# One pipeline over both images in layer 1, with the norms and copies moved into running work

## The chip, the cores and the metric

The kernel runs on one core of a Trainium2 chip, as one program. The time is the device time of one execution in microseconds (us). The core has a matrix engine (TensorE, PE in the profile; PEld is its loading of weights), a vector engine (VectorE, DVE), an engine for functions of one operand (ScalarE, ACT), a general engine (GpSimd, POOL) and an engine that here only issues transfers (SyncE, SP). Each engine works through its own queue in order. ScalarE can issue transfers too; such an issue stands in its queue between its other instructions.

## The reference

Two layers, each with a residual, on an input of 2 images of 64 x 64 places with 256 channels, all in float32:

```
x = x + L0(gn(x))        # gn: normalise over groups of 8 channels and all places of an image
x = x + L1(gn(x))

L0: mamba scans of rows (mh) and of columns (mv), each forward and backward:
    xz = x @ in_w.T;  xi, z = split(xz)
    xi = silu(conv4(xi)); dt, B, C = split(xi @ x_w.T); dt = softplus(dt @ dt_w.T + b)
    h_t = exp(dt*A) * h_{t-1} + dt*xi*B ;  y_t = sum_n h_t*C    # 16 states, 512 channels
    out = ((y + xi*D) * silu(z)) @ out_w.T ; the four results are joined by fc_w

L1: for i in 0, 1:
        x = x + mamba2(rmsnorm(x))   over columns ("t" weights of layer i)
        x = x + mamba2(rmsnorm(x))   over rows    ("b" weights of layer i)
    mamba2: one product with Win, conv4 and silu, decays exp(cumsum) as 64 x 64 matrices
            for 8 heads, both directions, gate, rmsnorm, product with Wout
```

L1 is four calls of mamba2 in a row; each needs the whole image of the call before, since columns and rows take turns. The two images never meet.

## The kernel before

Channels lie on the 128 partitions, in two groups (`KT`); an image is a tile of 128 x 2 x 4096. Two such tiles are held: `XU` (the layer's input, and in layer 1 the running `U`) and `Y` (layer 0's result).

A block is four rows or columns of 64 places (`TB` = 256 places); an image has 16 (`NBLK`). All work is cut into steps of a block. Lists such as `STEPS0` (layer 0) and `STEPS` (layer 1) give each step a due time within a block; `plan` adds block number times period, and `issue` sorts all steps by due time and emits them. So the order on every engine is written out by these numbers, and `pin` (keep in program order) fixes it. One block has a period of 3200 units in layer 0 (a step of the scan each 100) and of 100 in layer 1. Instructions that are not pinned may be moved by the framework that places the waits: the transfers of layer 1, and `group_norm` with what surrounds the calls there.

**Layer 0** (`layer0`) is one pipeline of 64 blocks: image 0 rows, image 0 columns, image 1 rows, image 1 columns. Per block and state, ScalarE makes the decay (L391), GpSimd the inflow (L741) or the product with C (L771), VectorE the scan (L760) or the product (L774), TensorE the sum over states (L398). The rows of B and C come from DRAM (`b_row`, `c_row`, issued by SyncE). Image 1's tile takes the place of image 0's as soon as the last `norm_x` (L570) of image 0 has read it: eight transfers (L418), issued one after the other on ScalarE's queue, then 16 `bn_stats` (L426) on VectorE and a chain of small operations to the factors `gscale` and `gshift`. Image 0's result is written to DRAM (`y_kept`, L471), likewise eight transfers one after the other on ScalarE's queue. `residual` (L854, L864) ends a block.

**Layer 1** (`layer1`) is called twice, image 1 in `Y` first, then image 0. It begins with `group_norm` (L336 to L355) and writes the normalised `Y` into `U` (L936, 16 instructions). Then come four calls, each with its own loading and scaling of weights (L950 to L991, the pool has two buffers of each), and its own `issue` of 16 blocks. In a block: `norm_squares` (ScalarE), `norm_total` (GpSimd, L1045), `norm_mean` (TensorE), `norm_factor`, `norm_scale` (VectorE, L1057, writes `xn`), projections (TensorE, L930), convolution (ScalarE L927, VectorE L1018), decays (GpSimd L1162, TensorE, ScalarE), `outputs` (TensorE), `gated` (VectorE L1269), the second norm and projection, `residual` (GpSimd L1314). In the fourth call `residual` also adds `U` to `Y` (L1317), writes the output from `Y`, and for the first of the two images loads the other's `Y` back from `y_kept` (L1320) into the same place.

Of the kernel before, what the change touches and what calls it, by code (L numbers as in the profile page):

```python
# [134 lines left out]
    (-8799, "load"),  # L135
    (-7899, "stats", 0),
    (-7824, "stats", 1),
    (-7749, "stats", 2),
    (-7674, "stats", 3),
    (-7599, "stats", 4),  # L140
    (-7524, "stats", 5),
    (-7449, "stats", 6),
    (-7374, "stats", 7),
    (-7299, "stats", 8),
    (-7224, "stats", 9),
    (-7149, "stats", 10),
    (-7074, "stats", 11),
    (-6999, "stats", 12),
    (-6924, "stats", 13),
    (-6849, "stats", 14),  # L150
    (-6774, "stats", 15),
    (-6629, "moments"),
    (-6554, "mean_sum"),
    (-6479, "mean_dev"),
    (-6404, "var_sum"),
    (-6329, "factor"),
    (-6254, "offset"),
)
SPILL = 899
# [58 lines left out]
    (460, "out_scale"),  # L218
    (559, "residual"),
)  # L220

# [7 lines left out]
def seqs(ap):  # L229

    return ap.rearrange("p (s l) -> p s l", l=L)
# [97 lines left out]
def group_norm(nc, k, pool, psum, src):  # L329

    n = NTOK // 512
    stats = pool.tile([P, KT, n, 6], F32, name="gn_stats")
    moments = pool.tile([P, KT, 2], F32, name="gn_moments")
    for kt in range(KT):
        for j in range(n):
            nc.vector.bn_stats(stats[:, kt, j, :], src[:, kt, j * 512 : (j + 1) * 512])  # L336
        nc.vector.bn_aggr(moments[:, kt, :], stats[:, kt, :, :].rearrange("p n s -> p (n s)"))
    mean = pool.tile([P, KT], F32, name="gn_mean")
    nc.vector.tensor_copy(mean, moments[:, :, 0])
    pm = psum.tile([P, 512], F32, name="ps_mm")  # L340
    nc.tensor.matmul(pm[:, 0:KT], lhsT=k.gavg, rhs=mean, start=True, stop=True)
    gmean = pool.tile([P, KT], F32, name="gn_gmean")
    nc.vector.tensor_copy(gmean, pm[:, 0:KT])
    spread = pool.tile([P, KT], F32, name="gn_spread")
    nc.vector.tensor_sub(spread, mean, gmean)
    nc.vector.tensor_mul(spread, spread, spread)
    nc.vector.tensor_add(spread, spread, moments[:, :, 1])
    pv = psum.tile([P, 512], F32, name="ps_mm")
    nc.tensor.matmul(pv[:, 0:KT], lhsT=k.gavg, rhs=spread, start=True, stop=True)
    std = pool.tile([P, KT], F32, name="gn_std")  # L350
    nc.scalar.activation(std, pv[:, 0:KT], AF.Sqrt, bias=k.eps_gn)
    scale = pool.tile([P, KT], F32, name="gn_scale")
    nc.vector.reciprocal(scale, std)
    shift = pool.tile([P, KT], F32, name="gn_shift")
    nc.vector.scalar_tensor_tensor(shift, gmean, -1.0, scale, ALU.mult, ALU.mult)  # L355
    return scale, shift


def layer0(tc, k, d, big, x, kept_ctx):
# [11 lines left out]
    with ExitStack() as ctx:  # L371
# [35 lines left out]
        class Image:  # L407


            def __init__(self, b):  # L410
                self.b, self.Y = b, None

            def load(self):
                self.X = big.tile([P, KT, NTOK], F32, name="XU")
                for j in range(NTOK // 512):
                    t = slice(j * 512, (j + 1) * 512)
                    queue = nc.scalar if self.b else nc.sync
                    pin(queue.dma_start(out=self.X[:, :, t], in_=x[self.b][:, :, t]))  # L418

            def stats(self, i):  # L420
                n = NTOK // 512
                if i == 0:
                    self.st = small.tile([P, KT, n, 6], F32, name="gn_stats")
                kt, j = i % KT, i // KT
                t = slice(j * 512, (j + 1) * 512)
                pin(nc.vector.bn_stats(self.st[:, kt, j, :], self.X[:, kt, t]))  # L426

            def moments(self):
                self.mom = small.tile([P, KT, 2], F32, name="gn_moments")
                for kt in range(KT):  # L430
                    st = self.st[:, kt, :, :].rearrange("p n s -> p (n s)")
                    pin(nc.vector.bn_aggr(self.mom[:, kt, :], st))
                self.mean = small.tile([P, KT], F32, name="gn_mean")
                pin(nc.vector.tensor_copy(self.mean, self.mom[:, :, 0]))

            def mean_sum(self):
                self.pm = ps_mm.tile([P, 512], F32, name="ps_mm")
                matmul(self.pm[:, 0:KT], k.gavg, self.mean, True, True)

            def mean_dev(self):  # L440
                self.gmean = small.tile([P, KT], F32, name="gn_gmean")
                pin(nc.vector.tensor_copy(self.gmean, self.pm[:, 0:KT]))
                self.spread = small.tile([P, KT], F32, name="gn_spread")
                pin(nc.vector.tensor_sub(self.spread, self.mean, self.gmean))
                pin(nc.vector.tensor_mul(self.spread, self.spread, self.spread))
                pin(nc.vector.tensor_add(self.spread, self.spread, self.mom[:, :, 1]))

            def var_sum(self):
                self.pv = ps_mm.tile([P, 512], F32, name="ps_mm")
                matmul(self.pv[:, 0:KT], k.gavg, self.spread, True, True)  # L450

            def factor(self):

                log = small.tile([P, KT], F32, name="gn_log")
                act(log, self.pv[:, 0:KT], AF.Ln, bias=k.eps_gn)
                self.gscale = small.tile([P, KT], F32, name="gn_scale")
                act(self.gscale, log, AF.Exp, scale=-0.5)

            def offset(self):
                self.gshift = small.tile([P, KT], F32, name="gn_shift")  # L460
                pin(
                    nc.vector.scalar_tensor_tensor(
                        self.gshift, self.gmean, -1.0, self.gscale, ALU.mult, ALU.mult
                    )
                )

            def spill(self):
                self.kept = big_dram(tc, kept_ctx, [P, KT, NTOK], f"y_kept{self.b}")
                for j in range(NTOK // 512):
                    t = slice(j * 512, (j + 1) * 512)  # L470
                    pin(nc.scalar.dma_start(out=self.kept[:, :, t], in_=self.Y[:, :, t]))  # L471
# [394 lines left out]
        images = [Image(b) for b in range(n_img)]  # L866
# [18 lines left out]
        todo += plan(images[1:], 2 * period * NBLK, shifted(IMAGE0, 2 * period * NBLK), -4)  # L885
        spill = [(2 * period * NBLK + SPILL, "spill")]
        todo += plan(images[:-1], 2 * period * NBLK, spill, -4)

        images[0].load()
# [6 lines left out]
        for _, name, *args in IMAGE0[1:]:  # L896
            getattr(images[0], name)(*args)
# [9 lines left out]
        return images[-1].Y, [image.kept for image in images[:-1]]  # L907


def layer1(tc, k, d, U, Y, out, after):  # L910
# [6 lines left out]
    with ExitStack() as ctx:  # L917
# [14 lines left out]
        gscale, gshift = group_norm(nc, k, small, ps, Y)  # L932
        for j in range(NTOK // 512):
            for kt in range(KT):
                t = slice(j * 512, (j + 1) * 512)
                nc.vector.tensor_scalar(  # L936
                    U[:, kt, t],
                    Y[:, kt, t],
                    gscale[:, kt : kt + 1],
                    gshift[:, kt : kt + 1],  # L940
                    ALU.mult,
                    ALU.add,
                )

        for call in range(4):
            ax, li = "tb"[call % 2], call // 2
            axis = "vh"[call % 2]

            w_in = wp.tile([P, KT, PROJ], F32, name="w_in")
            nc.sync.dma_start(out=w_in, in_=d[ax + "_Win"][li])  # L950
            w_out = wp.tile([P, CT, C], F32, name="w_out")
            nc.sync.dma_start(out=w_out, in_=d[ax + "_Wout"][li])
            norm_w = wp.tile([P, KT], F32, name="norm_w")
            nc.sync.dma_start(out=norm_w, in_=d[ax + "_norm_w"][li])

            cols = wp.tile([P, CT, TAPS + 3], F32, name="cols")
            nc.sync.dma_start(out=cols, in_=d[ax + "_cols"][li])
            bc_cols = wp.tile([P, TAPS + 1], F32, name="bc_cols")
            for j in range(2):
                nc.sync.dma_start(  # L960
                    out=bc_cols[j * NS1 : (j + 1) * NS1, :], in_=d[ax + "_bc_cols"][li][:, j, :]
                )
# [40 lines left out]
            def bank():  # L1003
                return ps.tile([P, 512], F32, name="ps_mm")
# [394 lines left out]
```

## Time and profile before

Three runs took 8777.42, 8782.16 and 8782.59 us; the median is 8782.16. The profiled execution has a span of 8783.1 us.

| | whole span | 5000 to 5100 us (layer 0) | 6450 to 6500 us (layer 1) |
|---|---|---|---|
| TensorE busy | 91% | 89.0% | 100% |
| its weight loads | 75% | 76.1% | 79.0% |
| VectorE | 87% | 97.7% | 75.1% |
| ScalarE | 80% | 84.7% | 80.3% |
| GpSimd | 89% | 99.9% | 77.7% |
| granted TensorE clock | 0.956 | 0.98 | 1.00 |
| moved by DMA | 109 GB/s | 149 GB/s | 1 GB/s |

How it is read: the shares of the whole span mix two stages with different limits, so each stage has to be read by itself. A busy TensorE is not TensorE at its peak, for matmuls overlap and their ends are modelled. Where one engine's instruction repeats once a block, its starts give the time of a block. "idle <- X" behind an instruction names what ended the wait of its engine.

Layer 0 lasts until its last `residual` starts at 6263.2 us; the rest is layer 1.

### The profile page before, as it was taken

How to read it: one execution, taken by the hardware profiler on the slowest of the kernel's cores; microseconds unless marked ns; L12 is line 12 of the kernel's file. 1: busy time of each engine (PE TensorE's matmuls, PEld its weight loads, DVE VectorE, ACT ScalarE, POOL GpSimd, SP SyncE). 2: the span in 40 equal slices, each digit the busy share in tenths (PEclk: the TensorE clock that was granted, in tenths of full speed). 3: DMA queues.
4: the chain of work that ended last, by engine and by line, in shares of the span. 5: the costliest groups of instructions: out<-in, count | busy, mean ns of one | idle time of the engine just before them, and what ended most of it. 6: DMA issues, size and time to landing. Idle time of an engine off the chain costs nothing. (4 is left out here: it accounts for less than half of the span.)

```text
span 8783.1 us, 150445 instructions
## 1 busy us (share of the span) xinstructions
PE 7950.0 (91%) x55632; PEld 6598.0 (75%) x55632; DVE 7651.9 (87%) x7433; ACT 7016.0 (80%) x12062; POOL 7787.5 (89%) x4494
## 2 busy tenths in 40 slices
PE   8989989898998889989988998998799999899999
PEld 6777777777777777777777777777677777677777
DVE  7999999999999989999999999999876666667666
ACT  6888888888888778888888888888577776677777
POOL 7999999999999899999999999999676666667667
PEclk9999999999999999999999999999899999999999
DMA  5444554544545554444554445555200000100000
GB/s 154 149 146 146 148 150 146 151 148 147 146 148 147 151 160 148 146 149 148 148 150 147 146 149 148 145 148 148 75 7 4 9 1 25 31 9 1 9 4 18
DMA packets 531631, 955.65 MB, mean 109 GB/s; under 512 B 71056, under 2 KB 83856, under 8 KB 528848
## 3 DMA queue, kind: packets, MB, share of 16 engines
q1 hardware_dynamic: 523568, 928.71, 36.0%
q10 hardware_dynamic: 7328, 17.31, 0.5%
q8 instruction: 440, 7.21, 0.3%
q14 instruction: 295, 2.42, 0.1%
HBM read 926.91 MB, written 18.87 MB: 108 GB/s over the span
## 5 line engine op out<-in xcount | busy, mean ns | idle before, releaser
L741 POOL TENSOR_TENSOR b<-dtx,b_row 128x1024 f32<-128x1024 f32 x1344 | 3161.2, 2373 | 12.5 <-DVE ps_h L760 12.3
L771 POOL TENSOR_TENSOR prod<-prod,c_row 128x1024 f32<-128x1024 f32 x1088 | 2565.0, 2369 | 69.7 <-DVE prod L760 67.9
L398 PE MATMUL ps_y<-ident,prod 128*128 128x128 f32 x16384 | 2141.7, 280 | 257.4 <-POOL prod L771 130.5
L398 PEld LDWEIGHTS ps_y<-ident,prod 128*128 128x128 f32 x16384 | 1889.1, 144 | 541.7 <-POOL prod L771 283.8
L391 ACT ACTIVATE ps_h<-dt,neg_a 128x512 f32<-128x512 f32 x2688 | 1847.6, 689 | 505.1 <-DVE prod L774 412.5
L760 DVE TENSOR_TENSOR_SCAN prod<-ps_h,b 128x1024 f32<-128x1024 f32 x960 | 2163.2, 2275 | 30.7 <-ACT ps_h L391 18.3
L760 DVE TENSOR_TENSOR_SCAN ps_h<-b,ps_h 128x1024 f32<-128x1024 f32 x576 | 1313.3, 2280 | 57.1 <-issue 34.7
L774 DVE TENSOR_TENSOR prod<-ps_h,c_row 128x1024 f32<-128x1024 f32 x960 | 1175.3, 1224 | 129.5 <-DVE ps_h L760 54.9
L391 ACT ACTIVATE scaled<-dtxt,bt 128x256 f32<-128x256 f32 x2560 | 1086.5, 495 | 239.6 <-PE ps_h L398 223.5
L930 PE MATMUL ps_mm<-xn,w_in 128*128 128x256 f32 x4608 | 1094.6, 388 | 25.7 <-DVE xn L1057 25.7
L1162 POOL TENSOR_TENSOR terms<-dta,within 128x512 f32<-128x512 f32 x512 | 523.3, 1044 | 611.7 <-DVE dta L1130 598.5
L930 PEld LDWEIGHTS ps_mm<-xn,w_in 128*128 128x128 f32 x4608 | 885.4, 195 | 161.0 <-DVE xn L1057 34.6
L391 ACT ACTIVATE b<-dt,neg_a 128x512 f32<-128x512 f32 x1408 | 929.4, 707 | 0.0
L394 PE MATMUL ps_mm<-xi,diag_w 128*128 128x256 f32 (+3 forms) x4096 | 918.3, 374 | 11.9 <-ACT dt L391 11.8
L398 PE MATMUL ps_h<-ident,scaled 128*128 128x128 f32 x5120 | 696.5, 280 | 246.4 <-DVE prod L760 226.9
L760 DVE TENSOR_TENSOR_SCAN ps_h<-ps_h,b 128x1024 f32<-128x1024 f32 x384 | 876.3, 2282 | 25.4 <-issue 12.0
L398 PEld LDWEIGHTS ps_h<-ident,scaled 128*128 128x128 f32 x5120 | 594.6, 145 | 398.4 <-ACT ps_h L391 292.7
L394 PEld LDWEIGHTS ps_mm<-xi,diag_w 128*128 128x128 f32 x4096 | 752.6, 190 | 90.4 <-ACT dt L391 12.1
L1018 DVE SCALAR_TENSOR_TENSOR conv<-ps_mm,cols,conv 128x252 f32<-128x252 f32 (+2 forms) x1536 | 705.3, 473 | 74.3 <-ACT conv L927 37.9
L394 PE MATMUL ps_mm<-xn,w_in 128*128 128x256 f32 x2048 | 546.2, 415 | 4.7 <-POOL xn L570 4.2
L927 ACT ACTIVATE conv<-ps_mm,cols 128x256 f32<-128x256 f32 x512 | 261.4, 561 | 296.7 <-PE ps_mm L930 296.5
L1269 DVE TENSOR_TENSOR yg<-ps_mm,gate 128x512 f32<-128x512 f32 x256 | 164.7, 685 | 382.8 <-PE ps_mm L930 382.8
(152 smaller groups left out, 12170.0 us busy)
## 6 DMA issues: line engine op xcount, KB each, us to landing
c_row<-bc_rows SPq DMA_DIRECT2D x2048, 256.0 KB, 3.5
b_row<-bc_rows SPq DMA_DIRECT2D x1344, 256.0 KB, 3.4
out_dram<-Y SPq DMA_DIRECT2D x32, 256.0 KB, 2.5
w_in<-in_L_t_Win_dram SPq DMA_DIRECT2D x4, 1160.0 KB, 5.1
w_in<-in_L_b_Win_dram SPq DMA_DIRECT2D x4, 1160.0 KB, 7.9
XU<-in_x_dram SPq DMA_DIRECT2D x8, 512.0 KB, 7.9
bc_rows<-dbc SPq DMA_DIRECT2D x64, 64.0 KB, 3.1
XU<-in_x_dram ACTq DMA_DIRECT2D x8, 512.0 KB, 10.6
```

Of the source, the lines that this page charges most:

```text
L391: pin(nc.scalar.activation(*args, **kwargs))
L394: pin(nc.tensor.matmul(out, lhsT=lhsT, rhs=rhs, start=start, stop=stop))
L398: nc.tensor.matmul(out, lhsT=x, rhs=order, start=start, stop=stop, is_transpose=True)
L741: pin(nc.gpsimd.tensor_mul(b, self.dtx[u], self.row(u, 0, n)))
L760: nc.vector.tensor_tensor_scan(*(t.rearrange("p c t -> p (c t)") for t in (to, a, b)), 0.0, ALU.mult, ALU.add,)
L771: pin(nc.gpsimd.tensor_mul(prod, prod, self.row(u, 1, n)))
L774: pin(nc.vector.tensor_mul(prod, self.h[u, n], self.row(u, 1, n)))
L927: pin(nc.scalar.activation(*args, **kwargs))
L930: pin(nc.tensor.matmul(out, lhsT=lhsT, rhs=rhs, start=start, stop=stop))
L1018: nc.vector.scalar_tensor_tensor(dsts[:, :, j:], pps[:, :, : L - j], w[:, TAPS - 1 - j : TAPS - j], dsts[:, :, j:], ALU.mult, ALU.add,)
L1162: nc.gpsimd.tensor_mul(terms, self.dta[:, s, :].unsqueeze(2).to_broadcast([P, NH, L]), k.within.unsqueeze(1).to_broadcast([P, NH, L]),)
L1269: pin(nc.vector.tensor_mul(yg5[:, :, :, e, :], py, gate5[:, :, :, e, :]))
```

## The change

*Layer 1 becomes one pipeline of 128 blocks* (8 x `NBLK`). The order of the calls is now: call 0 of image 0, call 0 of image 1, call 1 of image 0, and so on. A block finds its call, its image and its weights by its number. The weights of the four calls are objects with steps (`WEIGHTS`): a call's weights are loaded 15 blocks ahead and scaled in the first blocks of the call. Image 0's `U` is the tile `XU`, image 1's is the tile `Y`, in place.

*The norms leave the seam.* `group_norm` becomes a class `GroupNorm` with steps. Image 0's result, spilled to DRAM in layer 0, is loaded back into `XU` while layer 0 works on its last blocks (`again`), gets its statistics there, and is normalised in place by 16 `apply` on ScalarE. Image 1's is spilled to DRAM and normalised in place during the first 14 blocks of layer 1 (`NORM`), while those blocks work on image 0. The factor comes from a logarithm and an exponential everywhere.

*The residual of layer 1* takes layer 0's result from DRAM, 256 KB a block (`y_load`), for both images.

*Loads and spills in pieces.* In layer 0 the eight transfers of a load get due times of their own, 150 units apart (the first starting 250 after the last `norm_x`), those of the spill 250 apart.

The core of the diff:

```
 IMAGE0 = (
-    (-8799, "load"),
-    (-7899, "stats", 0),
...
-    (-6254, "offset"),
+    (-8609, "load", 0),
+    (-8459, "load", 1),
+    (-8309, "load", 2),
+    (-8209, "stats", 0),
+    (-8159, "load", 3),
...
+    (-7559, "load", 7),
...
+    (-6584, "offset"),
 )
-SPILL = 899
+APPLY0 = tuple((-6459 + 150 * i, "apply", i) for i in range(16))
+SPILL0 = tuple((1069 + 250 * j, "spill", j) for j in range(8))
...
+    (480, "y_load"),
     (559, "residual"),
 )
+WEIGHTS = (
+    (-1500, "load"),
+    (10, "scale_in", 0),
+    (20, "scale_in", 1),
+    (200, "decay_rates"),
+    (240, "diag_skip"),
+    (300, "scale_out", 0),
...
+NORM = (
+    *((20 * j, "spill", j) for j in range(8)),
+    *((260 + 30 * i, "stats", i) for i in range(16)),
+    (760, "moments"),
...
+    (910, "offset"),
+    *((950 + 30 * i, "apply", i) for i in range(16)),
+)
...
+    def apply(self, i):
+        kt, _, x = self.piece(i)
+        scale, shift = self.gscale[:, kt : kt + 1], self.gshift[:, kt : kt + 1]
+        self.pin(self.nc.scalar.activation(x, x, AF.Identity, scale=scale, bias=shift))
...
-        todo += plan(images[1:], 2 * period * NBLK, shifted(IMAGE0, 2 * period * NBLK), -4)
-        spill = [(2 * period * NBLK + SPILL, "spill")]
-        todo += plan(images[:-1], 2 * period * NBLK, spill, -4)
+        there = 2 * period * NBLK
+        todo += plan([images[1]], 0, shifted(IMAGE0, there), -4)
+        todo += plan([images[0]], 0, shifted(SPILL0, there), -4)
+        todo += plan([again], 0, shifted(IMAGE0 + APPLY0, 2 * there), -4)
...
-        gscale, gshift = group_norm(nc, k, small, ps, Y)
-        for j in range(NTOK // 512):
-            for kt in range(KT):
...
-        for call in range(4):
-            ax, li = "tb"[call % 2], call // 2
...
             def __init__(self, i):
-                self.i = i
-                self.us = seq_view(U, axis, i)
+                self.call, self.b, self.i = i // (2 * NBLK), i // NBLK % 2, i % NBLK
+                self.w = weights[self.call]
+                self.us = seq_view(U[self.b], "vh"[self.call % 2], self.i)
...
+            def y_load(self):
+                if self.call == 3:
+                    self.t = slice(self.i * TB, (self.i + 1) * TB)
+                    self.y = two.tile([P, KT, TB], F32, name="y_in")
+                    nc.sync.dma_start(out=self.y, in_=kept[self.b][:, :, self.t])
...
-            issue(plan([Block(i) for i in range(NBLK)], 100, STEPS))
+        weights = [Weights(call) for call in range(4)]
+        norm = Norm(nc, k, pin, small, bank)
+        norm.X = U[1]
+        todo = plan([Block(i) for i in range(8 * NBLK)], 100, STEPS)
+        todo += plan(weights, 2 * NBLK * 100, WEIGHTS, -8)
+        todo += plan([norm], 0, NORM, -4)
+        issue(todo)
```

## Prediction

> **What bounds the kernel now.** I read the page's row of slices first, then the engines' busy time in stretches of 50 and 100 us, then the starts of `norm_scale` (L1057, one per block of layer 1), then the waits at the seams. The slices:
>
> ```profile
> PE   8989989898998889989988998998799999899999
> DVE  7999999999999989999999999999876666667666
> POOL 7999999999999899999999999999676666667667
> ```
>
> Two stages are to be seen. For 28.5 slices (6263 us) VectorE and GpSimd are full: layer 0. In the rest only TensorE is: layer 1, eight calls of 16 blocks (four calls for image 1, then four for image 0). The stretches of layer 1 (columns: PE, PEld, DVE, ACT, POOL busy us, granted clock, DMA share, GB/s):
>
> ```profile
> 6450.00:6500.00 50.00, 50.00 (x386) 39.48 (x385) 37.53 (x83) 40.15 (x72) 38.87 (x36) 1.00 0.00 1
> 6550.00:6600.00 50.00, 39.08 (x358) 28.44 (x356) 24.46 (x51) 25.52 (x44) 33.00 (x30) 0.92 0.11 36
> 7450.00:7500.00 50.00, 46.79 (x419) 37.36 (x418) 29.45 (x67) 33.01 (x61) 29.31 (x28) 0.97 0.10 33
> 7500.00:7550.00 50.00, 28.44 (x242) 19.54 (x240) 23.32 (x53) 17.28 (x29) 32.69 (x30) 0.84 0.24 77
> ```
>
> Inside a call TensorE has no hole and the others are 75 to 80% busy; between calls all fall. The starts of `norm_scale` give the beat: 17.69 us from block to block inside a call, to 0.03 us, with the first three intervals of each call shorter (together 40 to 43, I take 42) and about 50 us across a seam:
>
> ```profile
> 6533.10 1.05 DVE L1057 TENSOR_TENSOR xn<-XU,ps_mm 128x512 f32<-128x512 f32 x1
> 6550.29 1.05 DVE L1057 TENSOR_TENSOR xn<-XU,ps_mm 128x512 f32<-128x512 f32 x1
> 6602.40 0.69 DVE L1057 TENSOR_TENSOR xn<-XU,ps_mm 128x512 f32<-128x512 f32 x1 [2.84 <-ACT ps_mm L927]
> ```
>
> From the first `norm_scale` of a call to that of the next it is 307.3, 303.8, 304.3, 357.1 | 304.7, 305.2, 302.6 us, and 303.1 from the last one to the end at 8783.1: 2488.0 in all. Sixteen beats are 283.0, so a call pays 20 to 24 us of filling and draining, and the fourth 74. There VectorE waits, in the middle of a call, for image 0's `Y` coming back:
>
> ```profile
> L336 DVE BATCH_NORM_STATS2 gn_stats<-Y 128x6 f32<-128x512 f32 x16 | 10.3, 684 | 54.5 <-DMA Y<-y_kept 54.5
> ```
>
> At the seam of the layers, TensorE stands from 6263.1 to 6296.1 but for four small matmuls:
>
> ```profile
> 6254.20 8.94 PE L394 MATMUL ps_mm<-yg,w_out 128*128 128x256 f32 x32
> 6276.10 0.56 PE L341 MATMUL ps_mm<-gn_mean,gavg 128*128 128x2 f32 x2 [12.96 <-DVE gn_mean L339]
> 6292.89 1.22 PE L930 MATMUL ps_mm<-total,mean_c 128*128 128x256 f32 x2 [13.53 <-POOL total L1045]
> 6296.15 3.78 PE L930 MATMUL ps_mm<-xn,w_in 128*128 128x256 f32 x8 [2.04 <-DVE xn L1057]
> ```
>
> In layer 0 a block takes 95.5 us (starts of `residual`). The blocks that end at 2994.4 and 3303.2 took 121.6 and 108.8. ScalarE's queue shows a transfer ahead of each hole:
>
> ```profile
> 2885.27 1.71 ACT L391 ACTIVATE scaled<-dtxt,bt 128x256 f32<-128x256 f32 x4 [13.15 <-DMA XU<-in_x_dram]
> 3212.56 1.28 ACT L391 ACT_TABLE_LOAD   x1 [14.60 <-DMA y_kept<-Y]
> ```
>
> **What the Trainium skill says.** (1) Perfetto Trace Analysis, Identifying the Most-Contended Engine: a matmul busy share is no measure of the distance to the roofline, the weight loads' share is better. The trace agrees that "50.00 of 50" is not the last word (weight loads 39.5 of 50); so I rest on the beat, which repeats to 0.03 us while every other engine has a fifth of its time free. (2) TensorE: Matmul & The Clock Gate, Part 1: an idle window of about 3.4 us drops the clock to half, and it returns after as much work. The trace agrees: 0.84 to 0.92 at seams, 1.00 inside calls. Fewer seams, fewer cold restarts; they are already in the 20 to 24 us. (3) DMA: Bandwidth & Descriptors, Issuing engines are not separate DMA queues: transfers of ScalarE's and SyncE's queues share the same 16 engines. The trace agrees: in the 5 us after 2885 the DMA share is 0.98, and the row loads behind it are late.
>
> **The change part by part.**
>
> *One pipeline of 128 blocks.* Steps and their offsets inside a block stay, so I keep the beat. A block of call c+1 needs all blocks of call c of its own image, the last of which is due at 1500+559=2059 of the 3200 units between these calls: no wait. From first to last `norm_scale` there are then 127 intervals: 42 + 124 x 17.69 = 2235.6 us. The tail after the last one is today's, 8783.1-8734.5 = 48.6. Sum 2284.2 against 2488.0: **-203.8**. The next calls' weights, loaded and scaled at a seam today (w_in 2 x 0.8 us, w_out 4 x 0.34 on VectorE, diag_d 1.0 on GpSimd), come 15 blocks ahead into engines with a fifth free: nothing.
>
> *No norm between the layers.* Today: statistics, two matmuls, 16 times L936 (7.4 us), then the first block. After, image 0's normalised copy is there when layer 0 ends. What remains: `w_in`, whose load waits for layer 0's last matmul (6263.2 in the trace, landing 5.1 us later), its scaling 2 x 0.81, `norm_scale` 0.87. First projection near 6271.5 instead of 6296.1: **-24.6**. The block's own norm chain (1.1+0.7+1.2+0.8 us) lies beside the load.
>
> *Image 1's norm inside layer 1* (blocks 0 to 13): 16 statistics of 0.68 and 16 `apply` on ScalarE. No row of before shows such an `apply`; the nearest with both operands per channel is `conv<-ps_mm,cols` at 0.56 for 256 columns. ScalarE: Activation LUTs, What ACT_TABLE_LOAD costs, has 0.833 ns a column and about 93 ns for each such operand; for the 256 columns it would say 0.585, so the trace agrees. 0.56 + 0.21 = 0.77 for 512, an estimate. One piece each 30 units (5.3 us), against 25% free on VectorE and 20% on ScalarE. If all was hidden: 0; if each piece delayed a matmul by its length: 16 x (0.68+0.77) = 23. I take **+3**, as a piece delays in-order neighbours now and then. The spill of image 1 (4 MB) and `y_load` (256 KB a block, landing in 3 us, asked for 79 units or 14 us ahead) use a DMA share that is near 0. `y_load` adds a wait on GpSimd at the last addition; queued behind it are the next block's `terms` and `weight`, for which TensorE and VectorE wait, but 14 us against 3 leaves none of it; the fourth call's stall (54 us) goes with L336, and is inside the -203.8.
>
> *Layer 0: loads in pieces.* The block ending at 2994.4 lost 26.1 us: 4.7 waiting for `norm_x` (L570), 8.4 issuing eight loads at once, 13 for statistics on a full VectorE (16 x 0.68, small ops 2). Singly and 250 units after `norm_x`, a load costs ScalarE about 0.6 us, at 15% free; what is queued behind it is the next decay, for which the scan on VectorE waits. Gain 0 to 13, I take **-11**. *Spill in pieces*: the block lost 13.5; gain 5 to 13.5, I take **-11**.
>
> *Layer 0: image 0 once more.* Eight loads, 16 statistics, the small chain, 16 `apply`. VectorE is 97% busy here and GpSimd 99%, so the statistics cost what image 1's cost: 13. The `apply` fall 150 units (4.5 us) apart: 16 x 0.77 = 12.3 us on ScalarE within 72, where 15% or 11 are free. Between 0 (ScalarE often waits for VectorE) and 12; I take 6. Together **+19**.
>
> Sum: -203.8 - 24.6 + 3 - 11 - 11 + 19 = -228.4. From the median of 8782.2: 8553.8; **8554**.
>
> **The rivals.** *A, layer 0 pays more:* pieces disturb a stage where two engines are full. With no gain from spreading (0 and -5), 25 for the second norm and 12 in layer 1: -203.8-24.6-5+25+12 = -196, **8586**. For it: 97 to 99% busy engines and a fixed order on each. Against: 4.5 us between pieces, and in today's trace single issues of 0.6 us in the same queue without a hole. *B, layer 1 loses its beat* in the 32 blocks with `y_load` and the 14 with the norm: today a wait on VectorE made the fourth call's blocks alternate 22.7 and 17.0, 2.2 over the beat on average: 46 x 2.2 = 101, **8655**. For it: GpSimd would wait in order behind a late load. Against: image 0's last call has the same extra addition and output, and keeps 17.69. *C, the seams stay* since the buffers of the two images or `U` as a whole tie the calls together: only the 74-21=53, and the 24.6, go, +8 for the norms: -70, **8712**. Against: inside a call, blocks read and write parts of one `U` without waits. *D, slower:* unbroken matmuls for 2.3 ms bring the granted clock down. At 0.85 the beat is 20.8: 124 x 3.1 = 386, less 228: **8940**. Against: 250 us at a time at 1.00 today, and 0.95 to 0.98 in layer 0 for 6 ms. *E, layer 0 gains more:* the `apply` free, statistics half hidden (-13 more): **8541**.
>
> **How the numbers follow.** Main case 0.58, A 0.17, E 0.10, B 0.08, C 0.03, D 0.04. The range must hold main, A and E with the bounds of the unknown costs: 8554 - 13 (all of E) - 11 (shorter fill, spills wholly free) = 8530 below; A's 8586 and a half-size B above, 8605. Faster by over 0.2% (below 8765): all but D, 0.95. Within: 0.01. Slower: 0.04.
>
> **What would show it.** Right: one run of `norm_scale` starts 17.69 apart over all 128 blocks; TensorE's slices of 9 from 6270 on with clock 1.0; first projection within 9 us of layer 0's last matmul; layer 0's holes near 2876 and 3202 gone, and one block near 6000 longer by some 15 to 20 us. Wrong: intervals above 17.69 in blocks 3 to 14 (the norm) or 96 to 127 (`y_load`), a clock under 1.00 in layer 1, or layer 0 ending after 6280.

## The result, and the profile after

The changed kernel takes **8562.35 us** (median of four runs, 8560.15 to 8563.57). Run beside it, the kernel before took 8779.79 (8771.87 to 8782.59). The ratio is 0.9753, with a 95% interval of 0.9737 to 0.977. The spans of the two profiled executions are 8783.1 and 8559.5 us, and the following shares out this difference of 223.6.

The slices of the page, first those of TensorE, VectorE and GpSimd:

```profile
PE   7989999899989889999998999899889999999999
DVE  7999999999999999999999999999977777777776
POOL 7999999999999999999999999999967777777777
```

The last ten slices lie wholly in layer 1. They have a flat 9 for TensorE, and for the others a flat 7 but for VectorE's last: the dents at the seams, where one call drains and the next fills, are gone. Two of the four stretches shown of before, with the same columns (PE, PEld, DVE, ACT, POOL busy us, granted clock, DMA share, GB/s):

```profile
6550.00:6600.00 50.00, 50.00 (x388) 39.51 (x385) 38.67 (x84) 39.42 (x71) 37.98 (x36) 1.00 0.01 2
...
7500.00:7550.00 50.00, 50.00 (x444) 39.29 (x443) 36.35 (x80) 39.46 (x69) 36.19 (x34) 1.00 0.01 1
```

Weight loads were 28.44 and 19.54 us in these two stretches before, where seams lay; now they are 39.5 and 39.3, as in the middle of a call. The clock is 1.00 and stays there from 6350 to 8500 us.

**Layer 1.** From the first `norm_scale` (now L1083) at 6265.85 to the last at 8509.04 there are 2243.2 us, and 50.4 from there to the end. Together 2293.6, against 2488.0 before: -194.4. From the 17th on the intervals are one beat, 17.69 us from block to block, but for those around the three changes of call. The first of these reads 19.05, 15.83, 21.17, 14.74, 17.58, 17.27: the sum is 105.6, half a microsecond under six beats, and the other two are as near. Where the next call's weight steps fall, one block comes late, and the next ones make it up. The wait in the middle of the fourth call is gone too. The 16 statistics of the image that comes second (L382, was L336) now lie in layer 1's own running work and waited 0.1 us in all; before, where the second image was loaded back, they had waited 54.5.

```profile
L382 DVE BATCH_NORM_STATS2 gn_stats<-Y 128x6 f32<-128x512 f32 x16 | 11.0, 685 | 0.1
```

**The seam.** From layer 0's last `residual` (L891) to the first `norm_scale` there were 31.9 us (6263.18 to 6295.08), now 8.4: -23.5. VectorE's timeline at the seam (start, busy us, instruction, then the idle time before it and what ended it):

```profile
6257.44 1.30 DVE L891 TENSOR_TENSOR Y<-ps_mm,Y 128x256 f32<-128x256 f32 x2 [7.54 <-PE ps_mm L470]
6264.37 1.56 DVE L998 TENSOR_SCALAR w_in<-w_in,norm_w 128x1160 f32<-128x1160 f32 x2 [5.63 <-DMA norm_w<-in_L_t_norm_w_dram]
6265.85 1.00 DVE L1083 TENSOR_TENSOR xn<-XU,ps_mm 128x512 f32<-128x512 f32 x1
6272.23 0.17 DVE L1139 TENSOR_TENSOR dt<-ps_mm,heads 128x16 f32<-128x16 f32 x1 [5.38 <-PE ps_mm L962]
6276.78 0.17 DVE L1016 TENSOR_SCALAR neg_a<-neg_a 128x8 f32<-128x8 f32 x1 [4.38 <-ACT neg_a L959]
...
6283.90 1.02 DVE L1083 TENSOR_TENSOR xn<-XU,ps_mm 128x512 f32<-128x512 f32 x1
```

and TensorE's:

```profile
6266.91 3.78 PE L962 MATMUL ps_mm<-xn,w_in 128*128 128x256 f32 x8 [7.29 <-DVE xn L1083]
...
6284.98 3.31 PE L962 MATMUL ps_mm<-xn,w_in 128*128 128x256 f32 x8 [4.63 <-DVE xn L1083]
```

What is left of the seam is the landing of the first weights and their scaling, as forecast (`w_in` landed 5.2 us after its issue; the small `norm_w`, issued behind it, landed 1.6 later and ended the wait). But the fifth line is a new wait. `decay_rates` (`neg_a`, L1016) stands in VectorE's queue ahead of the convolution of block 0 and waits 4.38 us for ScalarE; the next `xn`, behind it, comes late, and TensorE stands 4.63 us for that. The first three intervals are 18.05, 17.02 and 15.27 us, together 50.3 instead of the 42 that the forecast took from before. At the three later changes of call VectorE waits for the same step, 3.17 us each time, and there nothing is lost over six blocks, as the sum of 105.6 shows.

**Layer 0** now begins its last `residual` at 6257.4 instead of 6263.2. Around the change of image the ScalarE queue shows the loads one at a time:

```profile
2880.60 0.65 ACTq L494 DMA_DIRECT2D XU<-in_x_dram  x1
...
2884.66 0.55 ACTq L494 DMA_DIRECT2D XU<-in_x_dram  x1
2885.28 1.69 ACT L467 ACTIVATE scaled<-dtxt,bt 128x256 f32<-128x256 f32 x4
```

An issue costs 0.55 to 0.65 us, and the `scaled` behind it waits for nothing; the holes of 13.15 and 14.60 us are gone. The four blocks of the change of image took 121.6, 103.3, 96.8 and 108.8 us, and take 109.7, 102.4, 98.5 and 95.6: -24.3. Against that stands image 0's second norm in the last three blocks. The starts of their `residual`:

```profile
5965.63 1.38 DVE L891 TENSOR_TENSOR Y<-ps_mm,Y 128x256 f32<-128x256 f32 x2
...
6075.10 1.37 DVE L891 TENSOR_TENSOR Y<-ps_mm,Y 128x256 f32<-128x256 f32 x2
...
6172.98 1.31 DVE L891 TENSOR_TENSOR Y<-ps_mm,Y 128x256 f32<-128x256 f32 x2
```

with the 6257.44 above give 109.5, 97.9 and 84.5, in sum 291.8 against 279.3 before: +12.5. The first `residual` of all is 3.7 us later than before, and the rest of the 64 blocks differ by 2.4; both are within what layer 0 wanders between kernels that share it (its first `residual` began between 189.9 and 197.0 us in the traces of the kernels that follow). In sum: -194.4 - 23.5 - 24.3 + 12.5 + 3.7 + 2.4 = -223.6.

### The profile page after: what moved, and what is told of

It is laid out like the page before. It is cut to its first block, busy times and chain, and to the rows that moved or that the text cites. A ratio compares the mean times of both kernels' runs of the same rounds, so it can differ in the third digit from the quotient of the medians.

```text
span 8559.5 us, 150239 instructions
## 1 busy us (share of the span) xinstructions
PE 7881.5 (92%) x55632; PEld 6562.3 (77%) x55632; DVE 7631.3 (89%) x7371; ACT 7022.7 (82%) x12082; POOL 7776.3 (91%) x4490
## 5 line engine op out<-in xcount | busy, mean ns | idle before, releaser
L787 DVE TENSOR_TENSOR_SCAN prod<-ps_h,b 128x1024 f32<-128x1024 f32 x960 | 2164.4, 2276 | 19.3 <-POOL b L768 9.4
L962 PE MATMUL ps_mm<-xn,w_in 128*128 128x256 f32 x4608 | 1062.7, 380 | 13.4 <-DVE xn L1083 13.4
L962 PEld LDWEIGHTS ps_mm<-xn,w_in 128*128 128x128 f32 x4608 | 868.2, 191 | 128.4 <-DVE xn L1083 14.3
L470 PE MATMUL ps_mm<-xn,w_in 128*128 128x256 f32 x2048 | 549.2, 417 | 7.4 <-POOL xn L597 4.1
```

What stands on the lines that cost most here:

```text
L470: pin(nc.tensor.matmul(out, lhsT=lhsT, rhs=rhs, start=start, stop=stop))
L787: nc.vector.tensor_tensor_scan(*(t.rearrange("p c t -> p (c t)") for t in (to, a, b)), 0.0, ALU.mult, ALU.add,)
L962: pin(nc.tensor.matmul(out, lhsT=lhsT, rhs=rhs, start=start, stop=stop))
```

## The experiments

All kernels start from the changed one. A difference given as "in the trace" compares block times of the profiled executions, because layer 0's whole length wanders by some microseconds between kernels that have the same layer 0 (its last `residual` began between 6256 and 6270 us), and a few microseconds can't be read from the medians.

### One pipeline for each image and call, in the old order

This leaves the blocks, the weights as steps and the places of the norms, and undoes the taking of turns: image 0's four calls, then image 1's. Each call's steps are put behind those of the call before, so that it drains first, but not between the images. The weights are loaded for each of the eight calls.

```
-                self.call, self.b, self.i = i // (2 * NBLK), i // NBLK % 2, i % NBLK
+                self.call, self.b, self.i = i // NBLK % 4, i // (4 * NBLK), i % NBLK
...
+        for c in range(8):
+            start = 100 * NBLK * c + 460 * (c - c // 4)
```

> The changed kernel with one thing undone: in layer 1 image 0 makes its four calls first, then image 1, each call draining before the next of its image starts; weights still come 15 blocks ahead, norms stay where the change put them. Theory of the prediction (a seam costs 20 to 24 us because blocks of the next call need all of the last one): six seams come back, 6 x 21 = +126, 8562 -> about 8688. Rival (the seams cost what the late loading and scaling of weights cost, and order matters little): +0 to +40, below 8605.

Measured: 8725.58 (8722.26 to 8728.82), ratio to before 0.9937 (0.9922 to 0.9951): 163 us of the 217 are given back, 37 more than expected. The six seams are there again. TensorE's timeline at the first one:

```profile
6553.65 4.33 PE L962 MATMUL ps_mm<-terms,between 128*64 128x512 f32 x8 [3.23 <-POOL terms L1188]
...
6573.68 1.22 PE L962 MATMUL ps_mm<-total,mean_c 128*128 128x256 f32 x2 [5.40 <-POOL total L1071]
6576.63 3.78 PE L962 MATMUL ps_mm<-xn,w_in 128*128 128x256 f32 x8 [1.73 <-DVE xn L1083]
```

The last blocks of a call have no projections of later blocks between their own steps, so TensorE waits for each engine in turn; then it waits for the first `norm_total` of the next call. From call to call there are 309.5 to 314.9 us at the six seams, 26 to 32 over sixteen beats of 17.69 (283.0), where the kernel before had paid 20 to 24. So the main mechanism is shown: it is the filling and draining, six times, that the turns take away. What is over the forecast, some 6 to 7 us a seam, is dearer filling: after a seam the first three intervals sum to 48 to 52 us, not 40 to 43. So the 163 is what the old order costs with these weight steps, not what it cost before. At each of the six VectorE waits 2.8 to 4.6 us for `decay_rates`, as in the first filling of the changed kernel. That such a step causes a dearer filling is shown below for that one; for the six here it is inferred.

### Loads and spills in one go

```
+        bulk = [(-8799, *s[1:]) if s[1] == "load" else s for s in IMAGE0]
-        todo += plan([images[0]], 0, shifted(SPILL0, there), -4)
+        todo += plan([images[0]], 0, [(there + 899, "spill", j) for j in range(8)], -4)
```

> The changed kernel with image 1's eight loads issued at once right after image 0's last norm, and image 0's eight spills at once, as before; the second load of image 0 stays in pieces. Theory of the prediction: the pieces were worth 22 us (11 and 11), so 8562 -> 8584; from the block times of the two traces, 24. Rival (the transfers are hidden anyway, the change in the block times comes from elsewhere): +0 to +5.

Measured: 8584.1 (8581.63 to 8585.92), ratio 0.9775 (0.9761 to 0.979), 22 us slower than with the pieces. The four blocks take 120.2, 102.3, 98.4 and 107.6: +10.5 and +12.0 in the two blocks that the forecast named. ScalarE's timeline in the first of them:

```profile
2881.19 8.30 ACTq L494 DMA_DIRECT2D XU<-in_x_dram  x8
2889.54 1.71 ACT L467 ACTIVATE scaled<-dtxt,bt 128x256 f32<-128x256 f32 x4 [13.06 <-DMA XU<-in_x_dram]
```

Eight issues in a row cost ScalarE 8.3 us, and the `scaled` behind them waited 13.06 us again. The other 4.7 us of this wait lie ahead of the first issue, which stands in the queue until the last `norm_x` has read the tile. The edit takes back two things, the spacing and the later start (the first load 190 units, the spill 170), so the 22 us are the worth of both together; the spacing alone was not tried.

### Without the 16 `apply`, and without the whole second norm of image 0

```
-        todo += plan([again], 0, shifted(IMAGE0 + APPLY0, 2 * there), -4)
+        todo += plan([again], 0, shifted(IMAGE0, 2 * there), -4)
```

> The changed kernel without the 16 instructions of ScalarE that normalise image 0's copy in layer 0 (so layer 1 works on an image 0 that is not normalised; statistics are still made). Theory of the prediction: they cost 6 of the 19 us of the second norm, -6, 8556. Rival from the traces (two blocks longer by 12.5 in all, the statistics alone explain that): -0 to -2, 8560 to 8562.

```
+        todo += plan([again], 0, shifted([s for s in IMAGE0 if s[1] == "load"], 2 * there), -4)
```

> The changed kernel in which image 0 is loaded back in layer 0 and nothing else is done with it: no statistics, no factors, no normalising of image 0 for layer 1. Theory of the prediction: -19, 8543 (13 for statistics on a full VectorE, 6 for the normalising). Rival from the block times: -12.5, 8550. Rival (VectorE has room for them): -0 to -4.

Measured: 8564.56 (8558.57 to 8566.18), ratio 0.9751 (0.9735 to 0.9767), and 8549.29 (8544.6 to 8560.57), ratio 0.9738 (0.9723 to 0.9752). The last three blocks, in the trace: 109.5, 97.9, 84.5 in the changed kernel; 109.4, 94.3, 84.5 without `apply`; 99.0, 94.3, 83.6 without the norm. So the statistics and their small chain cost 10.4 in the first of the three blocks and 0.9 in the last, and the `apply` 3.6 in the second (97.9 in every kernel here with these `apply`). ScalarE's 16 `apply` are 12.8 us of work:

```profile
L432 ACT ACTIVATE XU<-XU,gn_shift,gn_scale 128x512 f32<-128x512 f32 x16 | 12.8, 802 | 1.5 <-DVE gn_shift L424 1.5
```

Three quarters of it are hidden, where the forecast had half of it shown.

### Image 1's norm left out of layer 1

```
-        todo += plan([norm], 0, NORM, -4)
+        todo += plan([norm], 0, NORM[:8], -4)
```

> The changed kernel without the statistics and the normalising of image 1 inside layer 1 (its spill stays; layer 1 works on an image 1 that is not normalised). Theory of the prediction: +3 for the norm, so 8559. Theory from the block times (blocks 4 to 14 take 194.4 us for 11 beats of 194.6; only the first three intervals can hold a cost): -0 to -4. Rival (each piece delays a matmul by its length): -23, 8539.

Measured: 8564.87 (8551.8 to 8571.12), ratio 0.9752 (0.9738 to 0.9765). The median tells nothing, as layer 0 ended 13 us later in the profiled execution. From first to last `norm_scale` the trace has 2240.9 us against 2243.2: the norm costs 2.3, all in the first three intervals (48.0 against 50.3). These three read 50.3 to 53.0 in the traces of six other kernels that leave the first blocks as they are, so the 2.3 is a rough size from one trace each. Blocks 4 to 14 take 194.4 us with the norm and 194.6 without; eleven beats are 194.6. The rival, that each piece delays a matmul by its length (23 us), is out.

### The filling cleared

First `decay_rates` alone is made 50 units (8.8 us) earlier; then, on top, the whole norm of image 1 starts 150 units later.

```
-    (200, "decay_rates"),
+    (150, "decay_rates"),
...
+        late = [(s[0] + 150, *s[1:]) for s in NORM]
```

> The changed kernel with one due time moved: the decay rates of a call (one exponential on ScalarE, its sign on VectorE) at 150 instead of 200, so that VectorE no longer waits for ScalarE between two convolution steps of block 0. Theory formed from the trace of the changed kernel (the first three intervals of layer 1 are 50.3 us instead of 42 because VectorE waited 4.4 us for this exponential and held the convolution): first three intervals near 46, time -4, 8558. Rival (the filling is slow because the spill of image 1 delays loads, or since the matrix clock is low): intervals unchanged, 8562.

> As the one before, and image 1's spill, statistics and normalising start 150 units (one and a half blocks) later, out of the filling of layer 1. Theory (the filling is slow by the extra steps on VectorE, of which the decay rates are half and the statistics some): first three intervals 42 to 44, time -7, 8555. Rival (only the decay rates matter): as the one before, 8558. Rival (neither): 8562.

Measured: 8560.92 (8555.06 to 8567.09), ratio 0.9749 (0.9736 to 0.9763), and 8554.82 (8550.65 to 8557.5), ratio 0.9742 (0.9728 to 0.9755). The first three intervals fall from 50.3 to 45.3, then to 44.4. The first step is more than the spread of 50.3 to 53.0 named above; the second, 0.9, is too small to be called shown. VectorE's timeline of the first of the two shows the wait of 4.38 us gone:

```profile
6271.84 0.17 DVE L1139 TENSOR_TENSOR dt<-ps_mm,heads 128x16 f32<-128x16 f32 x1 [5.30 <-PE ps_mm L962]
6271.93 2.90 DVE L1043 SCALAR_TENSOR_TENSOR conv<-ps_mm,cols,conv 128x252 f32<-128x252 f32 x6
```

In the medians a gain of 1 to 8 us is within what layer 0 wanders, so only the 5 us of the trace are claimed. The second of these kernels is the fastest here that computes the whole reference.

### Image 0's second statistics on ScalarE

On top of the cleared filling, VectorE's 16 statistics of image 0 become 32 ScalarE instructions (sum and sum of squares, accumulated as they pass), since VectorE is full in layer 0 and ScalarE is not. Two more things move with them: the small chain comes some 3700 units (a block and a fifth) later, and the 16 `apply` come behind it, 200 units apart, most of them in the last block. The lists of steps are left out here.

```
+                for n, func in enumerate((AF.Copy, AF.Square)):
+                    act(out.rearrange("p v q -> p (v q)"), x, func, accum_out=self.acc[:, n, kt, j : j + 1])
```

> As the one before, and the statistics of image 0's second norm are made on ScalarE (sum and sum of squares of each piece, 32 instructions of about 0.6 us, spread over two blocks) instead of VectorE. Theory from leaving the norm out (statistics cost 13 us because VectorE is full, ScalarE has 15% free and its 16 normalising instructions cost nothing): -11 to -13 against the one before, about 8543. Rival (any instruction put into layer 0's fixed orders costs its length, the free time on ScalarE is only waiting): 32 x 0.6 = 19 in place of 13, +6, about 8561.

Measured: 8563.39 (8557.86 to 8572.47, five runs), ratio 0.9754 (0.9741 to 0.9768): 8.6 slower than without this edit, not 11 to 13 faster. The last three blocks take 106.3, 113.6 and 84.2, 27 more than with no second norm at all. ScalarE's groups in this stretch (each with busy time, mean ns, and idle time before it):

```profile
L478 ACT ACTIVATE diag<-XU 128x512 f32<-128x512 f32 x32 | 20.1, 628 | 10.6 <-PE ps_h L481 10.0
...
L478 ACT ACTIVATION_READ_ACCUMULATOR diag<-XU 128x1 f32 x32 | 6.0, 186 | 0.0
```

Each accumulated sum brings a second instruction of 186 ns; together they are 26.1 us of ScalarE. It is tempting to set these 26.1 against the 27 and to call them not hidden at all, but the trace shows two other costs of the edit. The statistics write their unused output into a scratch tile, `diag`, of which there is one buffer, and the scan uses it too. Twice ScalarE stood until TensorE had read it:

```profile
6000.52 0.63 ACT L478 ACTIVATE diag<-XU 128x512 f32<-128x512 f32 x1 [5.74 <-PE ps_h L481]
...
6106.32 0.63 ACT L478 ACTIVATE diag<-XU 128x512 f32<-128x512 f32 x1 [4.31 <-PE ps_h L481]
```

And at its new place the small chain makes TensorE wait for VectorE, with the scan's matmuls behind:

```profile
6151.69 0.56 PE L407 MATMUL ps_mm<-gn_sums,gavg 128*128 128x2 f32 x2 [5.05 <-DVE gn_sums L917]
...
6161.28 0.58 PE L407 MATMUL ps_mm<-gn_spread,gavg 128*128 128x2 f32 x2 [5.36 <-DVE gn_spread L420]
```

Block by block, against the run without the second norm: in the first, 13.8 us of statistics and 5.7 of waiting for the scratch tile cost 7.3. The second, which has 12.2 us of statistics, the other wait and the chain, costs 19.3; VectorE's own work there is 8.7 us longer and its idle time 10.5 us. In the third, 11.2 us of `apply` cost 0.6. So the expected gain did not come, but the 27 us are not the price of the statistics alone. How much of them ScalarE can hide stays open: a kernel with a scratch tile of its own and the chain at its old place was not tried.

### The wait at `y_load`

Rival B of the prediction, a late load that GpSimd waits for with the next block's `terms` behind it, is tried in three sizes. First the load's due time alone is put off.

```
-    (480, "y_load"),
+    (558, "y_load"),
```

> In the 32 blocks of the last two calls the part of y_kept that a block adds to is now asked for 1 unit (0.2 us) ahead of the residual that needs it, not 79 units (14 us), with a landing of 3 us. So GpSimd waits in order about 3 us in each of these blocks, with the next block's terms queued behind it. The theory that only TensorE bounds this stage and that GpSimd has a quarter of its time free: 0 to +3 us, 8562 to 8565, and blocks 96 to 127 still 17.69 us apart. The prediction's rival B (a wait on GpSimd holds terms, and with them TensorE): 1 to 2 us a block, +32 to +64, 8594 or more, and intervals of 18.7 to 19.7 in these blocks alone.

Measured: 8562.79 (8554.01 to 8572.35), ratio 0.9746 (0.9729 to 0.9762). This is **no test**, for the load did not move. It is a transfer of layer 1, so it is not pinned, and its due time did not set its place before either. SyncE's instructions on `y_in` in the changed kernel, with the starts of the first and the last:

```profile
L1342 SPq DMA_DIRECT2D y_in<-y x32: 525/526/664, 6285.2 to 8548.9; - x32
L1349 SPq DMA_DIRECT2D out_dram<-y_in x32: 575/576/619, 8034.4 to 8555.9; - x32
```

The first two loads run at the start of layer 1, over 1740 us ahead of their additions. From then on each load waits for a buffer: `y_in` has two, so it starts when the output of two blocks earlier has landed, 2.5 us after that output's issue and 31.5 us, not the 14 us of the prediction, ahead of its own addition. The trace of this run has the same distances. (The weights moved likewise: those of the later calls were asked for a whole call, 32 blocks, ahead, not 15 blocks.) So the load is bound to the point of use instead, by a memset of one column on GpSimd ahead of it; in a third kernel it is made twice, one after the other.

```
             def residual(self):
...
+                    pin(nc.gpsimd.memset(self.y[:, :, 0:1], 0.0))
+                    nc.sync.dma_start(out=self.y, in_=kept[self.b][:, :, self.t])
```

> A late load for the 32 blocks of the last two calls: a memset of one column of y_in on GpSimd, ahead of the residual, holds the load back until that point. The load takes 3.0 us from issue to landing, the first addition 1.27, so GpSimd waits in order about 2 us in each of these blocks, with the next block's terms behind it. GpSimd waits 3.5 us a block for dta anyway. The theory that this free time takes it: 0 to +4 us, 8562 to 8566, blocks 96 to 127 still 17.69 apart, and the wait for dta down to about 1.5 us. Rival B of the prediction (a wait on GpSimd reaches TensorE): 2 us a block, +64, 8626, intervals of 19.7 in these blocks alone.

> The same with the load made twice, one after the other, so that GpSimd waits about 5 us in each of 32 blocks, 1.5 over the 3.5 that it has free. The theory that the free time is a buffer that can be used up: +1 to +2 us a block, +32 to +64, 8594 to 8626, intervals of 18.7 to 19.7 in these blocks. A theory that GpSimd is off the path altogether here, with slack of its own behind terms: 0 to +5, 8562 to 8567. Rival B (each us of waiting is paid): 5 us a block, +160, 8722.

Measured: 8568.99 (8560.49 to 8581.48), ratio 0.9761 (0.9745 to 0.9777), and 8613.09 (8604.49 to 8614.58), ratio 0.9809 (0.9794 to 0.9823). GpSimd's timeline with one load, around the wait:

```profile
8111.04 1.27 POOL L1350 TENSOR_TENSOR y_in<-y_in,XU 128x512 f32<-128x512 f32 x1 [1.91 <-DMA y_in<-y]
8113.92 4.20 POOL L1188 TENSOR_TENSOR terms<-dta,within 128x512 f32<-128x512 f32 x4 [1.61 <-DVE dta L1156]
```

and with two:

```profile
8119.44 1.27 POOL L1351 TENSOR_TENSOR y_in<-y_in,XU 128x512 f32<-128x512 f32 x1 [4.68 <-DMA y_in<-y]
8120.67 4.04 POOL L1188 TENSOR_TENSOR terms<-dta,within 128x512 f32<-128x512 f32 x4
```

With one load the new wait of 1.9 us is taken out of the old one: `terms` had waited 3.5 us for `dta`, and now waits 1.6. The 31 intervals from block 96 to 127 sum to 548.39 us in both the changed kernel and this one. The cost is in the last blocks, where nothing overlaps any more: 55.8 us from the last `norm_scale` to the end, for 50.4. With two loads the wait for `dta` is used up, and the 31 intervals sum to 579.9, 18.7 each. GpSimd's own work is 13.7 us a block (310.7 us in the 400 below); with the 4.7 of waiting it is 18.4, over the 17.69 at which TensorE has no hole. So the beat is the longer of two loops, TensorE's 17.69 and GpSimd's 13.7 plus what it waits for, and the forecast of +32 to +64 holds (31.5 in the beat, 15.1 in the tail).

The same stretch, 8000 to 8400 us, of the changed kernel:

```profile
8000.00:8400.00 400.00, 400.00 (x3447) 316.11 (x3437) 286.07 (x640) 307.02 (x566) 310.73 (x293) 1.00 0.09 29
```

and of the kernel with two loads:

```profile
8000.00:8400.00 400.00, 398.06 (x3290) 304.56 (x3289) 258.88 (x600) 295.16 (x537) 291.31 (x296) 1.00 0.13 39
```

TensorE's busy time says 398 of 400 in a kernel whose beat GpSimd sets and whose blocks are 5.7% longer. The Trainium skill (Perfetto Trace Analysis, Identifying the Most-Contended Engine) says that the busy share of matmuls is no good measure of how near a kernel is to its limit, and that the share of weight loads serves better. The trace agrees: the weight loads fell from 316.1 to 304.6 us, 3.6%, so they show the loss, if not all of it. The starts of `norm_scale` show it whole.

## Why the prediction was right, point by point

The forecast was 8554, and 8562 was measured; in the traces -223.6 us for the -228.4 forecast. That the sum is so near is in part luck: layer 1 gained 6.4 us less than forecast, image 0's second norm cost 6.5 less.

| step of the prediction | forecast | measured | from |
|---|---|---|---|
| one pipeline of 128 blocks, with image 1's norm inside | -203.8 + 3 | -194.4 | starts of `norm_scale` and the tail |
| of it image 1's norm | +3 | +2.3, roughly | the run without it |
| no norm between the layers | -24.6 | -23.5 | last `residual` to first `norm_scale` |
| loads and spill in pieces | -11 - 11 | -24.3 | blocks; -22 by the run that undoes it |
| image 0 once more | +19 | +12.5 | blocks; +14.9 by the run without it |
| not forecast: rest of layer 0 | 0 | +6.1 | first `residual` +3.7, other blocks +2.4 |

*One pipeline.* The mechanism was right and the beat was kept: 124 later intervals are at 17.69 on average (2192.9 for 2193.6). The term of the sum that was mis-sized is the first three intervals, of which it says "together 40 to 43, I take 42": they are 50.3. The sentence that failed is that the next calls' weights "come 15 blocks ahead into engines with a fifth free: nothing". For calls after the first that is so, as the sum of the intervals there shows. For the first call there is no running work: its `decay_rates` stands in VectorE's order ahead of block 0's convolution, and costs 5.0 us (the run that moves it). With the norm out of these blocks too, 44.4 are left. Of the 2.4 over 42, 1.4 lie in the choice of 42, for the first call of before took 43.4; the rest is within the spread. The tail is 50.4 for 48.6.

*Norm inside layer 1.* Right in size, as far as one trace each can tell, but it is paid only in the filling; once the pipeline runs, nothing is paid for 16 statistics and 16 `apply`. That "a piece delays in-order neighbours now and then" is true of single blocks and not of their sum. So intervals above 17.69 in blocks 3 to 14, which the prediction names as a sign of being wrong, did come (up to 20.23 us), and the next ones made them up.

*Image 0 once more.* The 13 for the statistics were about right (10.4 + 0.9 here by blocks). The 6 for `apply` were too much; 3.6 in the trace of one run without them, and none in the medians.

*Pieces.* Each at its forecast, to 1 or 2 us, if the spacing and the later start are taken together.

*The rivals.* A (layer 0 pays more) fell: spreading gave its full gain. B (layer 1 loses its beat at `y_load`) didn't come, and the two late loads show its size: by an estimate from 17.69 - 13.7, it would have taken some 4 us of waiting a block. It did not come since the loads were 31.5 us ahead, earlier than the prediction thought. C (the seams stay) came out near the old order's 8726 with its 8712, but by chance: that kernel has the 22 us of the pieces, which C left out, and the dearer fillings, which it did not know of. D (the clock falls) didn't come: 1.00 over more than 2 ms of unbroken matmuls. E (layer 0 gains more) came in part, in the `apply`.

## What to carry to other kernels

Where independent problems each run through a pipeline that fills and drains, let them take turns in one pipeline; the beat between the seams is the best forecast of what remains, and was kept here to 0.1%. The overhead measured at a seam, times their number, is the gain only if the new filling costs what the old one did; putting the six seams back cost 27 us each, not 21. An engine's free time is worth what it can wait without the beat noticing: compare its busy time and waits per block with the beat. GpSimd's 13.7 us and 1.9 of waiting were free, its 13.7 and 4.7 were not. When work is moved to a freer engine, look at what moves with it, its scratch tile and the chain that hangs on its result, before the engine is called full. Look last at the first block of the merged pipeline, the one place where steps made to lie beside other work have nothing to lie beside: a wait of 4.4 us for `decay_rates` was paid there, and waits of 3.2 us for the same step were not paid in the running pipeline.

## What the runs showed of the hardware that was not expected

- An accumulated sum on ScalarE is two instructions in the trace: 628 ns on average for 512 columns, and 186 ns for reading the accumulator.
- A transfer issued singly on ScalarE's queue took 0.52 to 0.65 us of it; eight in a row took 8.3 us, 1.0 each, and six of the spill in a row 10.2, 1.7 each. Back to back, an issue was dearer, and the next instruction of the engine stood behind it.
- Three of the small operations with which VectorE makes image 0's factors, on 2 or 4 columns, took 2.3 us each in the kernel with the statistics on ScalarE; two of the three, on `gn_spread`, took 0.16 us in the changed kernel. No run here shows why.
